# Layer 0 of a four-layer network: a new order of its operations, and the last tile's second-half sums on VectorE

## The chip, the cores and the metric

The kernel runs on one core of a Trainium2 chip. The metric is the device time in microseconds (us) of one execution, lower is better. A core has five engines with a queue each, which run in parallel and wait for each other through semaphores: TensorE (PE, with its weight load PEld), VectorE (DVE), ScalarE (ACT), GpSimd (POOL) and SyncE (SP), which issues most of the DMA transfers here. Every engine works strictly through its own queue: an instruction that waits holds up all that stand behind it.

## The reference

Four layers, each `x = x + layer(groupnorm(x))`, on x of 8 images, 16 channels, 256 x 256. Only layer 0 is touched. It is a capsule convolution with three rounds of routing:

```python
votes = conv3x3(groupnorm(x), w)          # 8 images, 8 atoms x 16 channels each
logits = zeros
for _ in range(3):
    r = softmax(logits, axis=images)
    preds = squash(sum over images, atoms kept: votes * r)
    logits = logits + sum over atoms: votes * preds
return preds
```

`squash(t)` is `n2 * t / ((1 + n2) * sqrt(n2))` with n2 the squared norm of t along its first axis. The softmax runs over the 8 images. Layers 1 to 3 (a spline convolution, an attention over patches, a circular convolution) follow and are the same in both kernels.

## The kernel before, in words

Layer 0 works on 64 tiles of four image rows, all images and channels at once. A tile has two halves, h = 0 and h = 1, of 512 columns for each partition. The first round needs no softmax (its logits are zero), so a tile goes through one squash, and then twice through "logits, softmax, weighted sum, squash". I call these two passes round 1 and round 2. The steps of a tile, with the lines that the profile names:

- Input: SP fetches x (`xs`, L478), PE normalises it (`pd`, two matmuls, L487), ACT moves it out (L490) and its queue puts it in DRAM (`d`, L499). This is made for tile i + 2 in the step of tile i.
- Votes: SP fetches shifted rows back (`kr` and `kt`, L528; `kt` of half 1, L610). Half 0: `cv<-kr` (L557, four matmuls) and `cv<-kt` (L550) for each of two row pairs; half 1: `cv<-kt` (L587 and L591), four operations of four matmuls. ACT copies them to `v` (L572, L596).
- Squash: ACT squares (L641), PE sums (`n`, L645, eight matmuls), ACT (L659 to L661), DVE (L665, L666), ACT (L670, L671), POOL (`times`, L675 to L678).
- Logits, for each half: PE spreads the factor over a PSUM buffer (`fb`, L697), DVE scales (L715) and multiplies twice (`pr`, L723, four and three images), PE sums (`pl`, L733, four and three matmuls). ACT moves `pl` out (L766 in round 1, L755 in round 2, where POOL adds it, L760).
- Softmax: PE transposes (`lg`, L780), DVE (L786, L787), ACT (L792), DVE (L796 to L798), PE transposes back (`rt`, L804), ACT copies (`rs`, L813).
- Weighted sum, for each half: PE spreads the weights in two groups, `rb45`+`r6` (three matmuls, L831) and `rb01`+`rb23` (four matmuls, L831); DVE makes four products `dd` (`dd45`, `dd6`, `dd01`, `dd23`, L842); POOL adds them up in five additions (L851): two of 128x1024 and three of 128x512.
- End: after round 2 a last `fb` for each half, DVE (L893), POOL (L896), ACT statistics (L908), SP stores.

PSUM holds three buffers of the kind "x" (two banks each) and two of the kind "u" (one bank each) for all of these; `pd`, `cv`, `fb` and `rb` each take an x buffer, the others a u buffer. A new use of a buffer waits for the last reader of the old one. So `fb`, for instance, can be held up by DVE still reading an older `rb`.

What comes when is not the order of this list. `work(i)` records each tile's 147 operations (`op`) with what they read and write, and `_Order.run` puts them in one sequence: operation m of tile n has the rank `n * 48 + TIMES[m]`, and among the operations whose predecessors are placed and whose buffers are free in the planner's count, the one of lowest rank comes next. The sequence is then cut up into the engines' queues. A negative entry of about -1000 stands for "as soon as it can". The durations given to `op` (its second argument) are not used by `run`. Two to three tiles are in work at once, so PE's queue for one period holds steps of three tiles.

Of the kernel before, what the change touches and what calls it, by code (L numbers as in the profile page):

```python
# [12 lines left out]
ALU = mybir.AluOpType  # L13
# [10 lines left out]
TILES = H // 4  # L24
# [160 lines left out]
class _Buf:  # L185
# [10 lines left out]


TIMES = [
    -1017.19, 743.46, 708.62, 498.18, -984.65, -996.51, -997.22, 751.01, 751.99, 751.01, 752.12, 750.77,
    -967.35, -903.62, -974.59, 753.99, 754.00, 753.77, 445.66, 393.73, -780.66, -960.80, 755.37, 755.59, 760.20,  # L200
    707.64, 775.69, 780.13, 782.25, 565.91, 658.76, 763.54, 681.24, 605.08, 709.84, 767.15, 644.09, 776.33,
    664.78, 790.04, 756.59, 796.59, 757.08, 765.74, 797.09, 318.31, 799.87, 800.80, 377.30, 696.72, 800.88,
    717.59, 571.56, 737.04, 802.63, 604.46, 530.71, 804.53, 784.88, 636.95, 657.50, 800.06, 517.07, 807.24,
    715.03, 742.15, 830.33, 840.65, 809.85, 812.29, 605.85, 802.98, 816.03, 807.95, 821.83, 824.88, 831.28,
    830.39, 840.66, 789.85, 845.72, 805.49, 748.11, 612.37, 736.06, 636.75, 809.44, 848.88, 838.39, 852.49,
    854.69, 850.98, 859.07, 855.18, 468.16, 857.49, 859.83, 859.02, 698.63, 610.89, 868.22, 704.59, 653.78,
    580.88, 884.00, 654.67, 695.12, 888.80, 889.83, 889.82, 808.47, 890.27, 690.66, 805.44, 696.48, 782.31,
    896.59, 899.53, 896.48, 777.07, 667.15, 682.59, 886.03, 640.00, 674.37, 898.75, 899.76, 887.82, 843.57,
    670.73, 902.64, 828.29, 828.95, 658.08, 885.55, 571.52, 801.95, -872.70, 907.37, 403.39, 814.67, 908.69,
    735.69, 919.60, 844.76, 829.08, -789.01  # L210
]


# [79 lines left out]
class _Net:  # L293
# [123 lines left out]
    def layer0(self, wd, bd, less0, tiles=range(TILES)):  # L417
# [5 lines left out]
        nc, tc = self.nc, self.tc  # L423
        xf = self.d["x"].rearrange("b c h w -> (b c) (h w)")
        last = B - 1
        with ExitStack() as st:
# [23 lines left out]
            for row in (0, H + 1):  # L450
                nc.sync.dma_start(
                    out=self.d0[row * ROW : row * ROW + ROW].rearrange("(p w) -> p w", p=P), in_=ring[0][:, 0, :]
                )
                nc.sync.dma_start(
                    out=self.x1[row and 15, :, :, row and 9, row and 1, :].rearrange("b c w -> (b c) w"),
# [3 lines left out]
                    out=self.x1p[:, row and 1, :, row and H // 2, :], in_=ring[0][:, 0, 0:W]  # L459
# [7 lines left out]
            def buf(kind, shape, name=None):  # L467
                pool = psum if kind in banks else sbuf
                n = {**places, **banks}[kind]
                return _Buf(kind, lambda: pool.tile(shape, F32, name=name or kind, tag=kind, bufs=n))  # L470
# [34 lines left out]
            def work(i):  # L505
# [3 lines left out]
                def op(*a, **k):  # L509
                    ops.append(order.op(*a, **k))  # L510
# [109 lines left out]
                def voted(h, a):  # L620
                    return [(v[h], a // 4, 0), (v[h], a // 4, 1)]
# [8 lines left out]
                def rows(ap):  # L630
                    return ap.rearrange("p (r w) -> p r w", w=W)
# [184 lines left out]
                def weighted(rs):  # L816


                    s = buf("s", [P, 2, 2, W])
                    for h in range(2):  # L820

                        def term(images, h=h):

                            rb = [buf("x", [P, 2, 512], "rb") if len(a) == 2 else buf("u", [P, 1, 512], "r6") for a in images]

                            def products():
                                for pair, r in zip(images, rb):
                                    for n, a in enumerate(pair):
                                        g, j = a // 4, (0, 2, 1, 3)[a % 4]
                                        at = slice(32 * j, 32 * j + 32)  # L830
                                        nc.tensor.matmul(  # L831
                                            r()[:, n], spread[at, g, h, :], rs()[at], start=True, stop=True
                                        )

                            op("PE", 1.25, products, [(rs, 0)], [(r, 0) for r in rb] + [(s, "turn")], mode="r32")
                            out = []
                            for pair, r in zip(images, rb):
                                n, a = len(pair), pair[0]
                                dd = buf("dd", [P, 2, 512])

                                def multiply(n=n, a=a, r=r, dd=dd):
                                    nc.vector.scalar_tensor_tensor(  # L842
                                        dd()[:, :n], r()[:, :n], 1.0 / B, v[h]()[:, a : a + n], ALU.subtract, ALU.mult
                                    )

                                op("DVE", 0.2 + 0.52 * n, multiply, [(r, 0)] + voted(h, a), [(dd, 0)])
                                out.append(dd)
                            return out

                        def add(out, a, b, us):  # L850
                            op("POOL", us, lambda: nc.gpsimd.tensor_tensor(out[0](), a[0](), b[0](), ALU.add),  # L851
                               a[1] + b[1], out[1])

                        d45, d6 = term([(4, 5), (6,)])
                        sh = (lambda h=h: s()[:, :, h], [(s, h)])
                        add(
                            sh,
                            (lambda h=h: rows(v[h]()[:, last]), voted(h, last)),
                            (lambda d=d6: rows(d()[:, 0]), [(d6, 0)]),
                            1.3,  # L860
                        )
                        d01, d23 = term([(0, 1), (2, 3)])
                        both = (d01, [(d01, 0)])
                        add(both, both, (d45, [(d45, 0)]), 2.4)
                        add(both, both, (d23, [(d23, 0)]), 2.4)
                        for n in range(2):
                            add(sh, sh, (lambda d=d01, n=n: rows(d()[:, n]), [(d01, 0)]), 1.3)
                    return s
# [1032 lines left out]
```

## Time and profile before

| what | value |
| --- | --- |
| time, median of 3 runs | 6140.17 us (6139.69 to 6145.74) |
| the profiled execution: time, span | 6146.27 us, 6144.5 us |
| PE busy over the span | 5840.8 us (95%) |
| DVE, ACT, POOL busy | 5267.0 us (86%), 3232.8 us (53%), 3815.2 us (62%) |
| in layer 0, 500 to 1000 us: PE, DVE, ACT, POOL busy of 500 us | 492.7, 454.4, 244.8, 440.2 us |
| the same stretch: granted PE clock, DMA share | 1.00, 0.54 |
| layer 0: first `pd`, last store issued | 100.9 us, 3274.5 us |
| layer 1: first matmul | 3296.9 us |

Layer 0 is thus some 3180 us of 6144. Its first 100 us are statistics of x, the next 150 us fill the pipeline, and from about 238 us the same pattern returns tile after tile until about 3150 us, when no further tile comes in and the engines run dry. A row of the timeline merges instructions of one line and tile that follow each other; the trace has two records for each of these matmuls, so `fb` with four matmuls is shown as x8. Its columns are: start, length, engine, line, operation, output and inputs, shapes, count, and in brackets idle time just ahead with what ended it.

### The profile page before, as it was taken

What the parts mean: (1) busy time and instruction counts of PE and PEld (TensorE: products, weight loads), DVE (VectorE), ACT (ScalarE), POOL (GpSimd) and SP (SyncE); (2) the same over time, 40 slices, a digit from 0 to 9 for tenths busy, and PEclk for the clock granted to TensorE, in tenths of its full rate; (3) what the DMA queues carried; (4) which work ended last, traced back from release to release, by engine and by line L of the source; (5) the groups of instructions that cost most, each with busy time, mean ns of one, the idle gap of its engine ahead of it and who ended that gap; (6) DMA issues with size and microseconds to landing.
All of it is one profiled execution on the core that took longest, in us unless ns stands there. A gap on an engine that the chain in (4) does not pass through costs nothing.

```text
span 6144.5 us, 117856 instructions
## 1 busy us (share of the span) xinstructions
PE 5840.8 (95%) x46024; PEld 2923.2 (48%) x46024; DVE 5267.0 (86%) x6933; ACT 3232.8 (53%) x4986; POOL 3815.2 (62%) x3552
## 2 busy tenths in 40 slices
PE   2999999999999999999976999999999999999998
PEld 0344444444444444444433444444444589999863
DVE  5799999999999999999987999999999877777741
ACT  0444454445444454445435888888888533333321
POOL 0588888888888888888884344434433344444333
PEclk9999999999999999999987999999999999999999
DMA  7455555555555555555524555555556554445458
GB/s 290 117 136 136 127 145 140 137 129 137 143 136 135 130 144 141 136 127 140 135 62 144 185 175 176 178 174 174 179 176 181 159 105 103 95 89 102 113 184 260
DMA packets 581531, 902.51 MB, mean 147 GB/s; under 512 B 292082, under 2 KB 368466, under 8 KB 537586
## 3 DMA queue, kind: packets, MB, share of 16 engines
q1 hardware_dynamic: 537138, 831.69, 49.8%
q10 hardware_dynamic: 33984, 34.08, 1.8%
q0 software_dynamic: 9856, 29.20, 1.6%
q8 instruction: 366, 6.00, 0.4%
q14 instruction: 187, 1.53, 0.1%
HBM read 684.09 MB, written 210.77 MB: 146 GB/s over the span
## 4 chain that ended last, share of the span: by engine, by line
PE 58%; DVE 27%; issue 7%; POOL 3%; DMA 3%; ACT 2%; SPq 0%; DVEq 0%; POOLq 0%; ACTq 0%
PE rb L831 8%; PE cv L587 7%; DVE bases L1089 7%; PE pq L1517 6%; PE pl L733 6%; DVE e L1079 5%; PE cv L591 4%; PE cv L550 4%; PE psc L1585 4%; PE po L1601 4%; PE p L1718 3%; PE pv L1517 3%; DVE pr L723 2%; DVE a L1079 2%; DVE a L1058 2%
## 5 line engine op out<-in xcount | busy, mean ns | idle before, releaser
L1112 PE MATMUL ps<-bases,tw 128*32 128x512 f32 (+1 forms) x13824 | 1360.6, 545 | 16.2 <-POOL bases L1081 6.5
L851 POOL TENSOR_TENSOR dd<-dd 128x1024 f32<-128x1024 f32 x512 | 1212.0, 2367 | 70.1 <-DVE dd L842 64.9
L1081 POOL TENSOR_TENSOR bases<-e,a 128x1024 f32<-128x1024 f32 (+1 forms) x264 | 621.7, 2378 | 926.4 <-DVE e L1079 926.4
L723 DVE TENSOR_TENSOR pr<-v,fb 128x2048 f32<-128x2048 f32 (+1 forms) x512 | 1020.8, 2014 | 17.1 <-PE pl L733 12.5
L1112 PEld LDWEIGHTS ps<-bases,tw 128*32 128x32 f32 x13824 | 597.6, 109 | 800.6 <-issue 484.2
L842 DVE SCALAR_TENSOR_TENSOR dd<-rb,v 128x1024 f32<-128x1024 f32 x768 | 906.8, 1215 | 8.8 <-POOL dd L851 3.3
L851 POOL TENSOR_TENSOR s<-s,dd 128x512 f32<-128x512 f32 x512 | 647.8, 1275 | 15.1
L831 PE MATMUL rb<-rs,ct_fold 32*128 32x512 f32 x3072 | 592.5, 634 | 25.6 <-DVE pr L723 20.1
L851 POOL TENSOR_TENSOR s<-v,dd 128x512 f32<-128x512 f32 x256 | 328.8, 1284 | 292.4 <-DVE dd L842 292.4
L587 PE MATMUL cv<-kt,w 128*128 128x512 f32 x1024 | 498.8, 609 | 11.6 <-DMA kt<-d 10.4
L733 PE MATMUL pl<-pr,ct_fold 128*32 128x512 f32 x3584 | 505.1, 601 | 3.1 <-DVE pr L723 3.1
L550 PE MATMUL cv<-kt,w 128*128 128x512 f32 x1024 | 477.3, 609 | 4.5 <-DMA kt<-d 4.5
L1089 DVE SCALAR_TENSOR_TENSOR bases<-xr,xm,bases 128x1024 f32<-128x1024 f32 (+1 forms) x264 | 446.5, 1729 | 0.3 <-POOL bases L1081 0.3
L596 ACT COPY v<-cv 128x1024 f32<-128x1024 f32 x256 | 251.9, 1008 | 303.3 <-PE cv L591 303.3
L1615 POOL COPY y<-y 128x2 f32<-128x2 f32 x128 | 24.1, 189 | 599.7 <-DVE y L1606 599.7
L1066 ACT ACTIVATE sq<-a 128x1024 f32<-128x1024 f32 (+1 forms) x264 | 263.7, 999 | 231.3 <-DVE a L1058 230.6
L831 PEld LDWEIGHTS rb<-rs,ct_fold 32*128 32x128 f32 x3072 | 226.0, 185 | 325.4 <-issue 129.1
L697 PEld LDWEIGHTS fb<-f,ct_fold 64*128 64x128 f32 x3072 | 208.3, 188 | 309.0 <-issue 176.6
L842 DVE SCALAR_TENSOR_TENSOR dd<-r,v 128x512 f32<-128x512 f32 x256 | 177.0, 692 | 191.3 <-PE r L831 176.8
L572 ACT COPY v<-cv 128x1024 f32<-128x1024 f32 x256 | 258.2, 1009 | 139.4 <-PE cv L550 139.3
L1048 ACT ACTIVATE d<-xr,bd,sd 128x1024 f32<-128x1024 f32 (+1 forms) x264 | 319.1, 1209 | 13.2 <-DMA xr<-x1p 13.2
L550 PEld LDWEIGHTS cv<-kt,w 128*128 128x128 f32 x1024 | 184.6, 190 | 289.1 <-issue 282.3
(320 smaller groups left out, 11365.5 us busy)
## 6 DMA issues: line engine op xcount, KB each, us to landing
xr<-x1p SPq DMA_DIRECT2D x120, 1024.0 KB
kt<-d SPq DMA_DIRECT2D x256, 387.0 KB
kt<-d SPq DMA_DIRECT2D x128, 516.0 KB
d<-dn ACTq DMA_DIRECT2D x64, 516.0 KB
kr<-d SPq DMA_DIRECT2D x128, 258.0 KB
kt<-d SPq DMA_DIRECT2D x128, 258.0 KB
x<-y SPq DMA_DIRECT2D x128, 258.0 KB
xs<-in_x_dram SPq DMA_DIRECT2D x16, 2048.0 KB
```

What stands on the lines that cost most here:

```text
L550: nc.tensor.matmul(ps[g]()[:, n], w[:, 0], t[:, a : a + 2, 0:W], start=False, stop=True)
L587: nc.tensor.matmul(ps()[:, n], w2[:, 0, j, :], t[:, a : a + 2, 0:W], start=True, stop=False)
L723: nc.vector.tensor_tensor(pr()[:, :n].rearrange("p n (r w) -> p n r w", w=W), v[h]()[:, 4 * g : 4 * g + n].rearrange("p n (r w) -> p n r w ...
L733: nc.tensor.matmul(pl()[at : at + 32], sel[:, g, h, :], pr()[:, t, :], start=h == 0 and g == 0, stop=h == 1 and (g == 1 or t == 3),)
L831: nc.tensor.matmul(r()[:, n], spread[at, g, h, :], rs()[at], start=True, stop=True)
L842: nc.vector.scalar_tensor_tensor(dd()[:, :n], r()[:, :n], 1.0 / B, v[h]()[:, a : a + n], ALU.subtract, ALU.mult)
L851: op("POOL", us, lambda: nc.gpsimd.tensor_tensor(out[0](), a[0](), b[0](), ALU.add), a[1] + b[1], out[1])
L1079: nc.vector.tensor_tensor(q, q, part[4 + k], ALU.mult)
L1081: nc.gpsimd.tensor_tensor(ring[n % 3][:, 0, p : p + m, 1 : 1 + W], rows(e), rows(a), ALU.subtract)
L1089: nc.vector.scalar_tensor_tensor(r, rows(part[1]), xm[:, b : b + 1], v, ALU.is_gt, ALU.mult)
L1112: nc.tensor.matmul(out if k is None else out[:, k], lhs, rhs, start=start, stop=stop, skip_group_check=True)
L1517: nc.tensor.matmul(out, lhs, rhs, start=start, stop=stop, skip_group_check=True)
```

## The change

Two edits, both in layer 0. The list `TIMES` gets 147 new numbers, said to be found with the transfers treated as a queue. And in the last tile (i = 63) the five additions of half 1 in each of the two rounds are issued on VectorE in place of GpSimd: ten instructions.

```diff
 TIMES = [
-    -1017.19, 743.46, 708.62, 498.18, -984.65, -996.51, -997.22, 751.01, 751.99, 751.01, 752.12, 750.77,
...
+    812.81, 884.95, 817.92, 666.13, -7133.44, -7210.22, -7230.57, 859.91, 871.57, 872.02, 854.18, 682.23,
...
 ]
...
-                        def add(out, a, b, us):
-                            op("POOL", us, lambda: nc.gpsimd.tensor_tensor(out[0](), a[0](), b[0](), ALU.add),
+                        name, engine = ("DVE", nc.vector) if h and i == TILES - 1 else ("POOL", nc.gpsimd)
+
+                        def add(out, a, b, us, name=name, engine=engine):
+                            op(name, us, lambda: engine.tensor_tensor(out[0](), a[0](), b[0](), ALU.add),
                                a[1] + b[1], out[1])
```

No instruction is added or removed. What the numbers do is seen in the queues that come out of them. In one period of the steady part PE's queue reads, from one `n` of a new tile to the next (the number behind a name is that of its matmuls, and `fb` has four):

```
before: n8 pl7 fb rb4 lg cv4 fb cv4 rt pd rb3 rb4 pl7 fb n8 kr4 kt4 rb3 rb4 pl7 fb lg kr4 kt4 rt
        cv4 rb3 rb4 n8 pl4 fb cv4 rb3 pl3 fb
after:  n4 fb n4 fb rb4 lg cv4 fb cv4 rt rb3 pl4 rb4 pl3 n8 kr4 fb kt4 rb3 rb4 pl7 fb lg kr4 kt4
        rt pd rb3 pl4 rb4 fb n8 pl3 cv4 cv4 rb3 pl7
```

(`kr4`, `kt4` are the operations of L557 and L550, `cv4` one of L587 and L591.) DVE's queue from the product behind the first `rb4` of that list on reads, in order:

```
before: dd01 | softmax | dd23 | softmax | scale pr4 pr3 | dd6 dd45 dd01 dd23 | scale pr3 ...
after:  dd23 | softmax | dd01 | softmax | scale pr4 pr3 | dd6 dd45 dd01 dd23 | f | scale pr4 ...
```

The `fb` that stands behind `pl7` (before) and behind `kr4` (after) there is the factor of half 1 in round 1. Before, its PSUM buffer is the one that `dd45` reads; after, it is the one that `dd23` reads, two products later in DVE's queue. `pd` stands between `rt` of round 2 and the `rb3` that needs its copy before; after, it stands behind `rt` of round 1, and `rt` of round 2 is followed by its own `rb3` at once. On SP, the fetch of `xs` stood at the head of the queue as early as the buffer allowed; now it stands among the others, and at the start of the layer the fetch of tile 1's x stands behind the six `kr` and `kt` fetches of tile 0.

## The prediction

> **What bounds the kernel now.** I read the busy shares in slices first, then the stretches of layer 0, then the timelines of PE and DVE over one tile, last the timelines of the run-out and of layer 1. From 500 to 1000 us PE is busy 492.7 of 500 us at full clock: layer 0 is PE's queue, and no transfer is waited for. The timeline of PE over a steady tile (start, length, ..., idle time ahead):
>
> ```profile
> 1570.99 0.65 PE L645 MATMUL n<-sq,ct_fold 128*32 128x128 f32 x16
> ...
> 1573.92 1.22 PE L831 MATMUL rb<-rs,ct_fold 32*128 32x512 f32 x8
> 1575.46 0.66 PE L780 MATMUL lg<-ct_fold,ls 128*128 128x128 f32 x4 [0.32 <-POOL ls L760]
> ...
> 1588.73 0.72 PE L697 MATMUL fb<-f,ct_fold 64*128 64x128 f32 x8
> 1589.37 0.65 PE L645 MATMUL n<-sq,ct_fold 128*32 128x128 f32 x16
> ...
> 1595.05 0.70 PE L831 MATMUL rb<-rs,ct_fold 32*128 32x512 f32 x2 [0.32 <-DVE pr L723]
> ...
> 1618.58 0.64 PE L645 MATMUL n<-sq,ct_fold 128*32 128x128 f32 x16
> ...
> 1621.50 1.22 PE L831 MATMUL rb<-rs,ct_fold 32*128 32x512 f32 x8
> ```
>
> The same `n` comes back after 1618.58 - 1570.99 = 47.59 us: the period. Cut it at two places: from `rb` x8 to `fb` 1588.73 - 1573.92 = 14.81 us (stretch A), from `fb` to the next `rb` x8 1621.50 - 1588.73 = 32.77 us (stretch B). PE's waits are 0.3 us long and two or three per tile, so there is little to gain: without them all, and with nothing else changed, at most 0.7 us per tile. What can be lost shows on DVE, in the same tile:
>
> ```profile
> 1575.17 1.22 DVE L842 SCALAR_TENSOR_TENSOR dd<-rb,v 128x1024 f32<-128x1024 f32 x1
> ...
> 1581.46 3.95 DVE L723 TENSOR_TENSOR pr<-v,fb 128x2048 f32<-128x2048 f32 x2
> 1585.84 0.69 DVE L842 SCALAR_TENSOR_TENSOR dd<-r,v 128x512 f32<-128x512 f32 x1 [0.42 <-PE r L831]
> 1586.44 3.48 DVE L842 SCALAR_TENSOR_TENSOR dd<-rb,v 128x1024 f32<-128x1024 f32 x3
> ```
>
> From 1575.17 to 1589.92 DVE has one pause, of 0.42 us. Today `fb` at 1588.73 waits for none of it: its buffer is free after `dd45`, the first of the three, at about 1587.66. The pause and this early release are what keeps DVE off PE's path.
>
> **The new order, stretch A.** In the new queue the same `fb` follows `kr4`, and its PSUM buffer is read last by `dd23`, the third of the three. DVE's row from the first `dd` to `dd23` keeps its members (first `dd`, softmax, second `dd`, softmax, scale, two multiplies, four `dd`), only the two first `dd` change places. Lay it out from the rows: `rb` x8 starts, the first `dd` 1.25 us later (1575.17 - 1573.92), the multiplies end 1585.41 - 1575.17 = 10.24 us after that, then the four `dd` take 1589.92 - 1585.84 = 4.08 us, without the pause, since `rb3` is now early. That is 15.57 us, less 0.08 of overlap, plus 0.05 to 0.15 for the hand-over (0.15 is how far `rb` at 1595.05 starts behind the end of its `pr`): A = 15.6 us, 0.8 more than today. What PE itself has to do there is less than before, since `pd` (1.81 us) has moved out: by its rows 14.3 us. So PE stands still for 1.3 us of A. Part of this is visible as a second wait. `rt` of round 2 is now followed by its own `rb3`, with no `pd` to cover ACT's copy. The rows of the run-out, where there is no `pd` left, price it:
>
> ```profile
> 3152.25 0.65 PE L804 MATMUL rt<-ct_fold,e 128*128 128x128 f32 x4
> 3153.93 0.70 PE L831 MATMUL rb<-rs,ct_fold 32*128 32x512 f32 x2 [1.03 <-ACT rs L813]
> ```
>
> There the copy waits some 0.35 us for ACT's previous copies; without these the idle time is 0.7 us. It lies inside A, so it is not added: if DVE were not late, it alone would remain. What is late next: behind `fb` on PE stand `kt4`, `rb` and all else, so the whole period shifts.
>
> **Stretch B.** It loses `n8` (1589.37 to 1589.95, 0.58) and `kr4` (1.08), which go to A, and gains `pd` (1.81): 32.77 - 0.58 - 1.08 + 1.81 = 32.92. The wait of 0.32 at 1595.05 falls away, but the `rb` behind such a wait run some 0.4 us faster (seven take 1.92 us there and 2.33 at 1584.55), so that gives nothing. New: `pl` and `rb` are cut into each other three times in a tile, and PE's queue has 45 runs for 43. `pl` as 4 and 3 takes 0.97 + 0.99 us where 7 take 1.85, so a cut costs 0.1; `rb` as 3 and 4 takes 1.06 + 1.22 against 2.30, so nothing. A second `rb` waits for ACT's copy out of `kt` (1.01 us and two hand-overs, against 0.96 us of PE work): 0.15. B = 32.92 + 0.1 to 0.5; I take 33.1. Between kinds of matmul that never follow each other in this trace the bounds are -0.3 (the cuts overlap) and +0.5; the row nearest to them, the cut `pl`, says 0.1 each.
>
> A + B = 48.7 us, against 47.59: **+1.1 us per tile**, bounds +0.4 (B at 32.6, and the bank free 0.3 earlier) and +1.5. Some 60 tile steps run so: +66 us.
>
> **Transfers.** In the steady part the fetches keep their lead: `kt` is fetched when its buffer is left by PE, and the new SP order puts nothing in front that waits longer than 18 us before the use; a burst of them took 7 us here. Cost nothing; if that cover went, every us late would be a us per tile. At the start SP's group `xs` x3 (97.05 us, 15.03 long) becomes one `xs`, six fetches that wait for tile 0's `d`, and only then tile 1's x: its fetch goes out near 113 us instead of 104.6, so its `pd` is 8 or more us later. Against that, tile 0's votes no longer stand behind the third `pd` (3.78 us at 115.05), and the fetch of half 1 no longer behind the put of tile 2, whose landing at 133.3 us held it. I take 0, bounds -6 and +8.
>
> **The last tile.** Ten additions go from POOL to DVE. POOL's rows in the run-out are 2.37 us (1024) and 1.28 us (512); for each round 2 x 2.37 + 3 x 1.28 = 8.6 us. DVE has no such row; the nearest are `dd` at 1.21 and `fb<-s,fb` at 0.69: 2 x 1.21 + 3 x 0.69 = 4.5 us. In round 2 of tile 63 POOL's chain runs from 3245.31 to 3263.30, 18 us, and the end waits for it. With both engines at once the end of half 1 would come near 3257.5, 5.8 us earlier. But these additions read two SBUF tiles, and in this trace such a DVE instruction does not run beside POOL's. Layer 1, two equal instructions:
>
> ```profile
> 3499.76 2.32 DVE L1089 SCALAR_TENSOR_TENSOR bases<-xr,xm,bases 128x1024 f32<-128x1024 f32 x1
> ...
> 3502.77 1.28 DVE L1089 SCALAR_TENSOR_TENSOR bases<-xr,xm,bases 128x1024 f32<-128x1024 f32 x1
> 3498.61 2.39 POOL L1081 TENSOR_TENSOR bases<-e,a 128x1024 f32<-128x1024 f32 x1
> ```
>
> The first has POOL beside it until 3501.00 and takes 2.32 us, the second has POOL idle and takes 1.28 us; L1079, with one operand in PSUM, takes 1.21 us either way. So 8.6 + 4.5 us go one after the other with about 1 us of waits: 14 us for 18, 4 us gained, and about as much in round 1, where POOL's queue is full from 3187 to 3223. I take -8, bounds 0 and -14.
>
> [...]
>
> **Sum.** +66 + 0 - 8 = +58 us. The profiled execution took 6146.27 us (span 6144.5 and 1.8 around it), so 6204 us; it lies 6.1 us above the median, and on the median of 6140.17 the forecast is **6198 us**, 1% slower. Bounds together: 60 x 0.4 - 6 - 14 = +4, and 60 x 1.5 + 8 = +98: 6144 to 6238.
>
> **Rivals.**
> - DVE is not the bound of A (the buffer is free earlier than the queue says), and only the uncovered `rs` copy remains: 0.7 of idle time less 0.2 that faster `rb` give back, +0.5 per tile; +30 - 8 = +22, 6162 us. For it: DVE's row has 1.3 us of play only by my sum of PE rows. Against: the hand-over is in the new queue. Chance 0.2; it lies in the range.
> - Faster: the waits of today vanish and no new one comes; PE runs at its rows. A at 14.3 plus B at 32.7 would be 47.0, -0.6 per tile: -36 - 8 = -44, 6096 us. It needs `dd23` to end 1.3 us sooner after `rb` x8 and the `rs` copy to be covered; it decides from A + B below 47.4. Against it: DVE's 15.6 us are rows, no estimates. For it: kinds of matmul in a sequence that the trace never shows. Chance 0.10.
> - No change: a period within 0.2 of today's, which A's excess and cheaper cuts could give, with the ends: about 6140. Chance 0.06.
> - The start goes wrong: tile 1's late x costs 8 to 15 us on top of the main case, 6210; in the range.
>
> Main case 0.64 and the first rival 0.2 are both slower by more than 0.2% (12 us, about what a measurement of this kernel can tell from no change). Faster 0.10, same 0.06, slower 0.84.
>
> **What would show it.** Right: a period near 48.7 us; PE idle before `fb` (L697), released by DVE `dd` L842, some 0.2 to 0.6 us in each tile, and before `rb` (L831), released by ACT `rs` L813, 0.7 us; POOL's chain at the end some 4 us shorter with DVE additions (L853) longer than 1.21 us; PE busy below 97% in the steady part. Wrong: a period at or below 47.6, or PE idle mainly on transfers.

## The result, and the profile after

| what | before | after |
| --- | --- | --- |
| median of 4 runs each, us | 6140.67 (6139.69 to 6145.74) | 6176.38 (6173.73 to 6181.34) |
| ratio to before | 1 | 1.0053, 95% interval 1.0041 to 1.0065 |
| span of the profiled execution, us | 6144.5 | 6171.9 |
| steady period, us | 47.59 | 48.05 |
| stretch A, stretch B, us | 14.81, 32.77 | 15.50, 32.54 |
| tile 2's `n`, us | 237.9 | 242.4 |
| tile 60's `n`, us | 2999.2 | 3028.2 |
| tile 63's `n`, us | 3141.0 | 3171.7 |
| last operation of layer 0 ends, us | 3276.1 | 3306.4 |

The change makes the kernel 0.53% slower. The lower rows say where: layer 0 ends 30.3 us later. Of these, 4.5 us are lost before tile 2's `n`, 24.5 us over the next 58 tile steps (0.42 us each in the mean), 1.7 us in the three steps after them, and 0.4 us come back behind tile 63's `n`. The layers behind, which are the same, took 2.9 us less in this execution than in the one of before.

PE's timeline over the same tile as in the prediction (start, length, engine, line, operation, output and inputs, shapes, count, idle time ahead and what ended it):

```profile
1586.80 0.41 PE L645 MATMUL n<-sq,ct_fold 128*32 128x128 f32 x2
...
1589.43 1.14 PE L831 MATMUL rb<-rs,ct_fold 32*128 32x512 f32 x8
...
1597.69 0.66 PE L804 MATMUL rt<-ct_fold,e 128*128 128x128 f32 x4
1599.03 0.70 PE L831 MATMUL rb<-rs,ct_fold 32*128 32x512 f32 x2 [0.68 <-ACT rs L813]
...
1601.09 1.14 PE L831 MATMUL rb<-rs,ct_fold 32*128 32x512 f32 x8
...
1603.58 1.35 PE L557 MATMUL cv<-kr,w 32*128 32x512 f32 x8
1604.93 0.72 PE L697 MATMUL fb<-f,ct_fold 64*128 64x128 f32 x8
...
1634.84 0.41 PE L645 MATMUL n<-sq,ct_fold 128*32 128x128 f32 x2
```

and DVE's in the same tile:

```profile
1600.81 0.68 DVE L842 SCALAR_TENSOR_TENSOR dd<-r,v 128x512 f32<-128x512 f32 x1
1601.41 3.47 DVE L842 SCALAR_TENSOR_TENSOR dd<-rb,v 128x1024 f32<-128x1024 f32 x3
...
1605.70 0.70 DVE L715 TENSOR_TENSOR fb<-v,fb 128x512 f32<-128x512 f32 x1 [0.43 <-PE fb L697]
```

The period is 1634.84 - 1586.80 = 48.04 us; A is 1604.93 - 1589.43 = 15.50. `fb` starts at 1604.93, 0.05 us behind the end of DVE's third `dd` (`dd23`, 1604.88), and yet no idle time stands ahead of it. The `kr` ahead of it was held up too: its row is 1.35 us long, where the same operation later in the tile takes 1.14. `kr` takes two PSUM buffers, and its third matmul, the first into the second buffer, starts at 1603.81, 0.06 us behind the end of `dd01` (1603.75). So PE waits for two of DVE's products in a row, and none of it is listed as idle time: a wait can lie inside a row, between the matmuls of one operation.

PE's waits from 1000 to 1500 us (us in total, times, longest), first before, then after:

```profile
PE lg L780 <- POOL ls L760: 3.6, 11, 0.3
PE rb L831 <- DVE pr L723: 3.5, 11, 0.3
```

```profile
PE rb L831 <- ACT rs L813: 6.7, 10, 0.7
```

Two waits of 0.32 us per tile have gone, and one of 0.68 has come. Such a list holds only the idle time between rows. Before had a hidden wait as well, in a `kr` of stretch B; PE's and DVE's rows there, then the same `kr` after:

```profile
1600.17 1.42 PE L557 MATMUL cv<-kr,w 32*128 32x512 f32 x8
...
1596.94 3.48 DVE L842 SCALAR_TENSOR_TENSOR dd<-rb,v 128x1024 f32<-128x1024 f32 x3
```

```profile
1614.69 1.14 PE L557 MATMUL cv<-kr,w 32*128 32x512 f32 x8
```

Before, the third matmul of this `kr` starts at 1600.47, 0.05 us behind the end of a `dd23` (1600.42); after, it is not held up. PE's work in a tile can thus not be had by taking the listed waits off the period. What changed in stretch B shows when every row is taken from its own start to the start of the next, so that waits are included (us, medians over the tiles from 600 to 2600 us):

| rows of stretch B | before | after |
| --- | --- | --- |
| first `kt`, the idle 0.32 us (before) and the seven `rb` behind it | 5.94 | 5.91 |
| the `kr` shown above | 1.35 | 1.07 |
| second `kt`, `rt` | 4.14 | 3.97 |
| the other ten `rb` | 3.36 | 3.20 |
| `cv` of half 1, twice | 5.85 | 5.95 |
| `pl` and `n`, 21 and 16 matmuls | 6.55 | 6.69 |
| `fb` five times, `lg` | 3.93 | 3.93 |
| `n8` and `kr4`, which go to A (before), `pd` (after) | 1.66 | 1.81 |

### The profile page after: what moved, and what is told of

Its sections match the earlier page's. It is cut to its first block, busy times and chain, and to the rows that moved or that the text cites. A ratio compares the mean times of both kernels' runs of the same rounds, so it can differ in the third digit from the quotient of the medians.

```text
span 6171.9 us, 118027 instructions
## 1 busy us (share of the span) xinstructions
PE 5845.4 (95%) x46024; PEld 2864.8 (46%) x46024; DVE 5293.9 (86%) x6943; ACT 3238.0 (52%) x4986; POOL 3817.4 (62%) x3542
## 4 chain that ended last, share of the span: by engine, by line
PE 51%; DVE 23%; POOL 16%; issue 5%; DMA 3%; ACT 2%; SPq 0%; POOLq 0%; ACTq 0%; DVEq 0%
PE cv L550 7%; DVE bases L1091 7%; PE rb L831 7%; PE pq L1519 6%; POOL dd L853 5%; PE pl L733 5%; DVE e L1081 4%; POOL s L853 4%; PE psc L1587 4%; PE po L1603 4%; PE p L1720 3%; PE pv L1519 3%; PE cv L557 2%; DVE a L1081 2%; DVE a L1060 2%
## 5 line engine op out<-in xcount | busy, mean ns | idle before, releaser
L853 POOL TENSOR_TENSOR dd<-dd 128x1024 f32<-128x1024 f32 x508 | 1199.4, 2361 | 101.6 <-DVE dd L842 81.7
L733 PE MATMUL pl<-pr,ct_fold 128*32 128x512 f32 x3584 | 522.3, 607 | 4.6 <-DVE pr L723 4.3
L587 PE MATMUL cv<-kt,w 128*128 128x512 f32 x1024 | 504.9, 615 | 9.5 <-DMA kt<-d 9.4
L550 PE MATMUL cv<-kt,w 128*128 128x512 f32 x1024 | 473.7, 605 | 2.5 <-issue 2.5
L831 PEld LDWEIGHTS rb<-rs,ct_fold 32*128 32x128 f32 x3072 | 162.5, 184 | 381.9 <-ACT rs L813 108.8
L1081 DVE TENSOR_TENSOR a<-a,sq 128x1024 f32<-128x1024 f32 (+1 forms) x264 | 312.3, 1183 | 2.3 <-ACT sq L1068 2.3
L1081 DVE TENSOR_TENSOR e<-e,sq 128x1024 f32<-128x1024 f32 (+1 forms) x264 | 312.3, 1183 | 0.0
```

The costliest lines, as they stand in the source:

```text
L550: nc.tensor.matmul(ps[g]()[:, n], w[:, 0], t[:, a : a + 2, 0:W], start=False, stop=True)
L587: nc.tensor.matmul(ps()[:, n], w2[:, 0, j, :], t[:, a : a + 2, 0:W], start=True, stop=False)
L733: nc.tensor.matmul(pl()[at : at + 32], sel[:, g, h, :], pr()[:, t, :], start=h == 0 and g == 0, stop=h == 1 and (g == 1 or t == 3),)
L831: nc.tensor.matmul(r()[:, n], spread[at, g, h, :], rs()[at], start=True, stop=True)
L853: op(name, us, lambda: engine.tensor_tensor(out[0](), a[0](), b[0](), ALU.add), a[1] + b[1], out[1])
L1081: nc.vector.tensor_tensor(q, q, part[4 + k], ALU.mult)
```

## The experiments

In some runs the planner's finished sequence is edited before it goes into the queues. An entry `([(a, m)], where, k, q)` puts operation m of tile n + a behind or ahead of operation q of tile n + k, for n from 5 to 59. Where there is no entry, the sequence is the planner's own.

**1. Is it DVE's chain that holds `fb`?** `dd6` of half 0 in round 2 is made twice:

```diff
-                                    nc.vector.scalar_tensor_tensor(
+                                    for _ in range(2 if last_round and h == 0 and n == 1 else 1):
+                                        nc.vector.scalar_tensor_tensor(
```

> The new order, and in each tile VectorE makes the product dd6 of half 0 in round 2 twice (0.61 us more; the values are the same). DVE has some 4 us of play per tile, so this costs something only where DVE is the bound. Theory (stretch A is set by DVE's unbroken chain up to dd23, which fb waits for): all of it is seen, A 15.5 + 0.6 = 16.1 us, period 48.65 us, time 6176 + 60 x 0.6 = 6212 us, ratio 1.011. Rival (the first rival of the prediction: only the uncovered rs copy holds PE in A, fb's buffer is free in time): period 48.05 us, 6176 us, ratio 1.005.

Measured: 6223.65 us, ratio 1.0128 (1.0113 to 1.0144), period 48.77. DVE's timeline of the doubled product:

```profile
1620.90 1.41 DVE L843 SCALAR_TENSOR_TENSOR dd<-r,v 128x512 f32<-128x512 f32 x2
```

It takes 1.41 us for 0.69, and the period grows by the same 0.72. On PE it is the `kr` ahead of `fb` that gets longer, from 1.36 to 2.08 us from its start to that of `fb`. DVE has 4 us of pauses in each tile, none of them on this stretch. So DVE's chain decides when PE gets to `fb`. The opposite, a chain made shorter, with VectorE scaling 64 columns of 512:

```diff
-                            nc.vector.tensor_tensor(p()[:, :, 0:W], s(h), p()[:, :, 0:W], ALU.mult)
+                            r, c = (1, 64) if h == 0 and before is None else (2, W)
+                            at = p()[:, 0:r, 0:c]
+                            nc.vector.tensor_tensor(at, s(h)[:, 0:r, 0:c], at, ALU.mult)
```

> The new order; VectorE scales only 64 of the 512 columns of fb for half 0 in round 1 (L715), so that its chain in stretch A is some 0.55 us shorter. The rest of that scaling is left out of the computation. Theory (DVE's chain up to dd23 holds fb some 0.3 us beyond the time at which PE, with its wait of 0.68 us on the rs copy, would be there): A falls from 15.50 to 15.2 us and the period to 47.75 us, no further, since PE's own row then sets it. Rival (only the rs copy is felt): period 48.05 us.

Measured: period 47.84, A 15.31 (a single execution took 6167.04 us, one of before beside it 6155.15). DVE's timeline of this run in A:

```profile
1591.84 0.22 DVE L717 TENSOR_TENSOR fb<-v,fb 128x64 f32<-128x64 f32 x1
...
1597.96 2.35 DVE L844 SCALAR_TENSOR_TENSOR dd<-rb,v 128x1024 f32<-128x1024 f32 x2 [0.18 <-PE rb L833]
```

0.47 us are saved on DVE and 0.20 are seen. The rest stands as a pause of 0.18 ahead of `dd01`, which now waits for PE's second `rb`. So two rows lead to `fb` and are within 0.2 us of each other: DVE's chain, and PE's own, `rs` copy, `rb3`, `pl4`, `rb4`, then `dd01` and `dd23`. I had looked for 0.30, with PE's row ending at `kr` and not in these two `dd`.

**2. Can the uncovered `rs` copy be covered again?** `pd` goes back between `rt` of round 2 and its `rb`:

```diff
+MOVES = [([(1, 0)], 'behind', -3, 143), ([(1, 1)], 'ahead', -2, 107), ([(1, 2), (1, 3)], 'behind', 0, 29)]
```

> The new order, but in the steady part pd (with its fetch of x and its copy) stands where it stood before: between rt of round 2 and the rb that needs the copy. Theory (PE's work is 46.9 us per tile in both kernels; after has 1.16 us of waits: 0.68 on the rs copy of round 2, some 0.3 on dd23 ahead of fb, 0.18 elsewhere; before has 0.69): the two waits of round 2 go, but the rs copy of round 1, which pd covered, comes out with 0.67: period 46.9 + 0.67 + 0.18 = 47.75 us, time near 6158 us, ratio 1.003. Rival 1 (the rs copy of round 2 is the whole loss, that of round 1 hides behind other work): 47.1 to 47.4 us, 6119 to 6137 us. Rival 2 (DVE's chain up to dd23 sets the stretch whatever PE does in it, and the cuts of pl and rb cost the rest): no better than 48.0 us, 6176 us.

Measured: 6191.5 us, ratio 1.0075 (1.0059 to 1.0090), period 48.32: slower than after, on the side of rival 2. PE's and then ACT's timeline of this run, further on in the tile:

```profile
1627.20 0.60 PE L824 MATMUL rt<-ct_fold,e 128*128 128x128 f32 x4
1628.96 0.70 PE L851 MATMUL rb<-rs,ct_fold 32*128 32x512 f32 x2 [1.15 <-ACT rs L833]
...
1627.40 1.01 ACT L592 COPY v<-cv 128x1024 f32<-128x1024 f32 x1 [0.70 <-PE cv L570]
1628.31 0.59 ACT L833 COPY rs<-rt 128x512 f32<-128x512 f32 x1
```

The copy of round 1, which `pd` had covered, now costs 1.15 us, since ACT is at a copy of `cv` when `rt` ends. And in A `pd` pushes the second `rb` back by a microsecond, `dd23` ends 0.8 us later, and A grows to 16.29 us. The next run takes away the part that is ACT's:

```diff
+MOVES = [([(1, 0)], 'behind', -3, 143), ([(1, 1)], 'ahead', -2, 107), ([(1, 2), (1, 3)], 'behind', 0, 29), ([(1, 19)], 'behind', 0, 56)]
```

> As the run with pd moved back, and ACT copies rs of round 1 ahead of the second copy of cv, behind which it stood (34.40 against a rt that ended at 33.89, in a tile's own time). That run had a period of 48.32 us with 1.15 us of idle time ahead of the rb of round 1. Theory (the copy waited 0.5 us for ACT): the idle time falls to 0.67 and the period to 47.85 us. Rival (PE would wait as long elsewhere, since the second copy of cv now comes 0.6 us later, or DVE's chain sets the period): 48.2 us or more.

Measured: period 48.30 (a single execution took 6182.80 us). The wait fell from 1.15 to 0.67 as said, and the period did not follow: it came back as waits for DVE, 0.21 us ahead of the second `rb` of round 1, whose buffer a `pr` still reads, and for POOL's `f`, 0.28 us ahead of an `fb`. With a second cover, `cv` behind `rt` of round 1:

```diff
+MOVES = [([(1, 0)], 'behind', -3, 143), ([(1, 1)], 'ahead', -2, 107), ([(1, 2), (1, 3)], 'behind', 0, 29), ([(1, 22)], 'ahead', 0, 57), ([(1, 23)], 'behind', -2, 129)]
```

> As the run with pd moved back, and the first cv of half 1 (2.94 us of PE work) is moved between rt of round 1 and the rb that needs its copy. Theory: both rs copies are covered, PE has 46.9 us of work and 0.1 to 0.4 us of waits: period 47.0 to 47.3 us, time near 6120 us, ratio 0.997, faster than both kernels. Rival (DVE's dd behind that rb now start 2.1 us later and DVE has only 4.2 us of play per tile, so DVE or its hand-overs set the period): 47.6 us or more, 6149 us or slower.

Measured: 6284.48 us, ratio 1.0223 (1.0209 to 1.0237), 49.84 us per tile in the mean. PE's waits from 1000 to 1500 us of this run:

```profile
PE fb L717 <- POOL f L698: 18.3, 17, 1.6
```

Both copies are covered and none of their waits is left, but the `dd` of round 1 come later, POOL's additions and its `f` behind them too, and PE waits for that instead. Both fills put PE work ahead of an `rb` and with it delayed DVE, which had none to spare there. The last run joins this case and the shorter DVE chain:

> The run with pd moved back and rs of round 1 copied first (period 48.30 us), with the same scaling of 64 of 512 columns, the rest of it left out of the computation. Theory (in that run DVE's chain sets the period, in A and behind fb, and PE follows it): nearly all of the 0.55 us is seen, 47.75 to 47.9 us. Rival (PE's wait of 0.67 us on the copy and its own row set it, DVE has play): 48.2 us or more.

Measured: period 48.75 (a single execution took 6210.92 us). By its number that is the rival's side, but the shorter chain made it slower than without, which neither side has a reason for. Of PE's waits from 1000 to 1500 us one is new, that of `rb` for DVE's `pr`, 0.36 us in each tile. In this build `rb3` was given the PSUM buffer that the second `pr` still reads, where in the run before it was the next `rb` that got it. The order of the operations is the same, the choice of buffers is not. Inconclusive.

**3. What does a cut of `pl` cost?**

```diff
+MOVES = [([(-2, 90)], 'ahead', -2, 92)]
```

> The new order, but in stretch B one of the cuts is undone: the pl of tile n-2 that stands as 4 and 3 with rb4, fb and n between goes out as 7 behind n. Theory (a cut costs nothing; stretch B was 32.55 us because the removed wait of 0.32 us was saved in full): the period does not fall; the rb that moves up waits 0.1 us for DVE's pr, so 48.05 to 48.2 us. Rival (the prediction's term, 0.1 us for each cut): 47.95 us.

Measured: period 48.29 (a single execution took 6191.65 us), 0.25 more with one cut less, which is more than either side expected. Of PE's waits from 1000 to 1500 us a new one:

```profile
PE rb L851 <- DVE pr L743: 1.8, 11, 0.2
```

Taken from start to start, `n8` and `pl7` in one take 2.28 us where the cut rows took 2.42, so the cut by itself costs 0.14 us, close to the prediction's 0.1. But the two `rb` that now follow each other take 2.52 us in place of 2.14: the `pl4` between them had given DVE the time to free the second one's buffer. Of these 0.39 us only 0.16 per tile (1.8 over 11) are listed as a wait. The net is the 0.25. The theory's reason, that the wait of 0.32 us had been saved in full, does not hold either: by the first row of the table above it gave 0.03.

**4. The start.** Tile 1's x is fetched ahead of tile 0's rows. The edit moves one operation, once:

```diff
+    o = at[(-1, 143)]
+    line.remove(o)
+    line.insert(line.index(at[(0, 14)]), o)
```

> The new order, but at the start of the layer the fetch of tile 1's x is put ahead of tile 0's kr and kt fetches on SP. Theory (this fetch alone makes the start late): its pd comes near 111 us in place of 127.4, the first votes of half 1 near 147 us in place of 154.2, tile 2's n near 238 us in place of 242.4; time 6176 - 4.5 = 6172 us. Rival (the third x, which the last kt fetch of tile 0 stands behind, or the burst of fetches takes it back): tile 2's n still at 240 us or later, 6174 us or more. The steady period stays at 48.05 us.

Measured: 6158.07 us, ratio 1.0020 (1.0011 to 1.0029), steady period 48.04. PE's timeline of the start, after and then this run:

```profile
127.36 3.78 PE L487 MATMUL pd<-xs,wd 128*128 128x512 f32 x4 [23.17 <-DMA xs<-in_x_dram]
...
154.19 3.75 PE L587 MATMUL cv<-kt,w 128*128 128x512 f32 x4 [9.39 <-DMA kt<-d]
```

```profile
107.80 3.65 PE L510 MATMUL pd<-xs,wd 128*128 128x512 f32 x4 [3.29 <-DMA xs<-in_x_dram]
...
141.30 1.96 PE L610 MATMUL cv<-kt,w 128*128 128x512 f32 x4 [1.38 <-DMA kt<-d]
```

The mechanism is the expected one, its size is not: tile 2's `n` comes at 226.8 us, 15.6 earlier than after and 11.1 earlier than before. One misplaced fetch had hidden that the rest of the new start is much the better one.

**5. The last tile.** The additions alone, in each of the two orders:

```diff
-                        name, engine = ("DVE", nc.vector) if h and i == TILES - 1 else ("POOL", nc.gpsimd)
+                        name, engine = "POOL", nc.gpsimd
```

> The new order of operations, with the ten additions of the last tile back on POOL. Theory (from the trace of after: from the first dd of round 1 in the last tile to the end of the layer takes 68.2 us with DVE additions, 73.1 us in the kernel before): the DVE additions save about 5 us, and the new order loses about as much ahead of that stretch. Then this kernel is 5 us slower than after, near 6181 us (ratio to before 1.0066), and that stretch takes 73 us. Rival (additions on DVE and POOL exclude each other, so that nothing is saved, and the shorter stretch comes from the new order): no change, 6176 us, stretch 68 us. In both the steady period stays at 48.05 us.

Measured: 6174.79 us, ratio 1.0046 (1.0034 to 1.0059), not to be told from after. From tile 63's `n` to the end of the layer it takes 136.4 us, after 134.7.

```diff
-    812.81, 884.95, 817.92, 666.13, -7133.44, -7210.22, -7230.57, 859.91, 871.57, 872.02, 854.18, 682.23,
...
+    -1017.19, 743.46, 708.62, 498.18, -984.65, -996.51, -997.22, 751.01, 751.99, 751.01, 752.12, 750.77,
```

> The old order of operations, with the ten additions of the last tile on DVE. Theory: 5 us faster than before, 6136 us (bounds 2 to 8 us faster), steady period 47.59 us, and the stretch from the first dd of round 1 in the last tile to the end of the layer 68 us in place of 73.1. Rival (the exclusion eats the gain): 6140 us, stretch 73 us.

Measured: 6150.02 us, ratio 1.0005 (0.9996 to 1.0014); the same stretch takes 139.8 us, before 135.1: longer, not shorter. I had compared the stretch from one row to the end across two orders, and laid a difference of the orders at the additions' door. Taken by rounds, in us (round 1 from tile 63's `n` to the first `dd` of round 2, round 2 from there to the start of the last `n`):

| run | order, additions on DVE | round 1 | round 2 |
| --- | --- | --- | --- |
| before | old, none | 103.6 | 19.5 |
| all ten, old order | old, ten | 111.1 | 16.7 |
| five, old order (below) | old, round 2 | 105.9 | 16.7 |
| five, old order, new start (below) | old, round 2 | 102.8 | 16.7 |
| back on POOL | new, none | 103.6 | 20.75 |
| after | new, ten | 105.2 | 17.5 |
| tile 1's x first | new, ten | 103.7 | 17.5 |

Round 2 gains 2.8 and 3.3 us. Round 1 gains nothing, and in the old order loses some 5 to 8 us. DVE's timeline there, in the run with the old order:

```profile
3199.85 0.70 DVE L787 TENSOR_TENSOR lg<-lg,e 128x512 f32<-128x512 f32 x1
...
3201.59 2.48 DVE L853 TENSOR_TENSOR dd<-dd 128x1024 f32<-128x1024 f32 x2
3204.10 0.69 DVE L853 TENSOR_TENSOR s<-s,dd 128x512 f32<-128x512 f32 x1
3204.71 0.68 DVE L796 TENSOR_REDUCE e<-lg 128x64 f32<-128x512 f32 x1
```

The additions stand in the middle of the other chain's softmax, 3.2 us of them between its two steps (L787, then L796), and the rest of that chain waits for it. What makes up the remainder of the 5 to 8 us is not shown. So only round 2:

```diff
-                        name, engine = ("DVE", nc.vector) if h and i == TILES - 1 else ("POOL", nc.gpsimd)
+                        name, engine = ("DVE", nc.vector) if h and i == TILES - 1 and last_round else ("POOL", nc.gpsimd)
```

> The old order, with the additions of the last tile's half 1 on DVE in round 2 alone (five instructions). In the run with all ten on DVE, round 2 of the last tile got 2.8 us shorter (from its first dd to the last n 16.7 us against 19.5) and round 1 7.5 us longer, since they stood in front of DVE's softmax. Theory: layer 0 ends 2.8 us earlier after tile 63's n than before (132.3 us against 135.1), time 6140.7 - 3 = 6138 us, ratio 0.9995, too little for these intervals. Rival (the gain of round 2 was only what round 1 had lost): 135 us.

Measured: 6142.22 us, ratio 0.9997 (0.9989 to 1.0006). Round 2 has the 2.8 us, but the end comes 134.6 us after tile 63's `n`: round 1, whose order is that of before, took 2.3 us longer (more on this below).

**6. What is good of it, on the old order.** The five additions as in the run before, and the start in the manner of run 4:

```diff
+    o = at[(0, 0)]
+    line.remove(o)
+    line.insert(line.index(at[(0, 13)]) + 1, o)
...
```

In the same way operation (0, 1) is put behind (0, 16), (0, 2) behind (0, 18), (0, 3) behind that, and (1, 0) behind (1, 4): the third x, its `pd`, copy and put stand behind tile 0's votes of half 0, and the fourth x behind tile 1's first rows.

> The old order in the steady part, additions of the last tile's half 1 on DVE in round 2 alone, and at the start the order of the run with tile 1's x first: two x fetches, then tile 0's kr and kt fetches, and the third x with its pd behind tile 0's votes. Theory (with the start as in that run, whose first votes of half 1 came at 141.3 us against 147.1 before): 6 to 11 us saved at the start and 3 in the last tile: tile 2's n near 230 us in place of 237.9, time ratio 0.998 to 0.9985, faster than both kernels. Rival (the fill of the old order waits for the third x, whose pd now comes some 20 us later): tile 2's n at 237 us or later, ratio 0.9995 or more.

Measured: 6136.31 us, ratio 0.9989 (0.9980 to 0.9998): faster than before by a tenth of a percent (the interval ends at 0.9998), between theory and rival. Tile 2's `n` is at 233.7 us (4.2 earlier than before, less than the 6 looked for), the period 47.59, and the end 131.5 us after tile 63's `n`.

## Why the prediction was right and where it was wrong

The sign, and the reason for it, held: slower, since A grows by DVE's chain and by a copy that nothing covers. Forecast +58 us; layer 0 in the traces shows +30, the medians +36. Term by term:

- *PE bounds layer 0, at most 0.7 us per tile to gain.* The 0.7 counts the idle time between PE's rows; the `kr` of before holds another 0.28 inside its row. No run here had a period below 47.59 us, so what there is to gain stays open.
- *A = 15.6 us.* Right: 15.50, and the two runs of experiment 1 show that DVE's chain sets it, so the first rival's reason (`fb`'s buffer is free in time, only the copy is felt) falls, though its +0.5 per tile is close to the measured 0.45. What I missed is that PE's row through `rb4` and the two last `dd` is only 0.2 us shorter: the 14.3 us of its rows left out the wait for the copy. And `kr4`, which moved ahead of `fb`, waits for `dd01` on its own.
- *B = 33.1 us.* This is the term that was mis-sized: 32.54. The sum reached 32.92 by moving operations and added 0.1 to 0.5; the rows give 0.4 less than 32.92. The largest piece is `kr`: the one that leaves was taken at 1.08, and the other was left at the 1.35 of before, which held a wait for DVE that the new order does not have (0.28 us). The ten other `rb`, one pair of them now cut by `pl`, took 0.16 less, where the sum put nothing, and the second `kt` with `rt` 0.17 less. The cuts of `pl` and `n` cost 0.14 in all (the sum had 0.1 each), and `cv` took 0.10 more. The wait of 0.32 was rightly booked as no gain: 5.94 us with it, 5.91 without. With B at 32.5 and A as forecast the period would have been 48.1, and the sum 60 x 0.5 = +30 in place of +66.
- *Start 0, bounds -6 and +8.* The net of +4.5 lies inside, but it is +15.6 from tile 1's x and -11.1 from the rest (run 4). I had put the late `pd` at 8 us or more; it came 19.4 us later than before.
- *Last tile -8.* Measured -0.4 for the whole run-out. In round 2 the additions save 3.3 us in this order (forecast 4), while DVE's and POOL's hold each other up (2.21 us for 0.69, 3.98 for 2.61), as the forecast had read it from the two rows of layer 1 (2.32 us for 1.28). "About as much in round 1" is the step that failed: I saw a full POOL queue and did not ask what the end of that round waits for, which is DVE's softmax.
- *What would show it.* The idle time ahead of `rb` came as said (0.68 against 0.7). The one ahead of `fb` is not listed, since the `kr` ahead of it was held up by DVE as well, and PE's busy share from 500 to 1000 us is 98.2% (490.9 of 500), not below 97%: such a share counts a wait inside a row as work.

Part of the miss cancelled by luck: the steady part was forecast 40 us too long (66 against 26), the start and the last tile together 12 us too short.

## What to carry to other kernels

Here two engines hand work back and forth, and the period followed the ring and not the busier engine's sum: before filling a gap on one engine, follow what the fill delays on the other. Add a known time to a suspected chain and see whether the period takes all of it; this settled in one run what the idle columns did not show. And ask of work moved off a full queue what its stage ends with, for a queue that is full is not always waited for.

## What the runs showed of the hardware

In round 2 of the last tile the additions on DVE and POOL held each other up, in both directions. DVE's and POOL's timelines there, in after:

```profile
3282.99 2.21 DVE L853 TENSOR_TENSOR s<-v,dd 128x512 f32<-128x512 f32 x1
...
3286.37 1.23 DVE L853 TENSOR_TENSOR dd<-dd 128x1024 f32<-128x1024 f32 x1
...
3279.88 4.77 POOL L853 TENSOR_TENSOR dd<-dd 128x1024 f32<-128x1024 f32 x2 [1.00 <-DVE dd L842]
3284.73 3.98 POOL L853 TENSOR_TENSOR s<-s,dd 128x512 f32<-128x512 f32 x2
```

DVE's addition of 512 columns, 0.69 us when alone, takes 2.21 while POOL's runs on to 3284.65. Then POOL's pair, 2.61 us elsewhere, takes 3.98: 1.37 more, with DVE's addition of 1.23 us inside.

In the run-out the same order does not take the same time. The two runs with the additions of round 2 alone, with the old start and with the new, have the same order of operations there, and need 134.6 and 131.5 us from tile 63's `n` on. The windows of each, twenty us at the same place, 28 us behind that `n` (stretch, its length, then the busy time of PE, PEld, DVE, ACT and POOL, granted clock, DMA share, GB/s), old start first:

```profile
3168.00:3188.00 20.00, 13.80 (x88) 5.87 (x82) 15.17 (x16) 4.40 (x10) 14.63 (x12) 0.70 0.00 1
```

```profile
3164.70:3184.70 20.00, 13.10 (x93) 5.80 (x90) 17.05 (x18) 4.41 (x10) 15.95 (x13) 0.83 0.00 1
```

and one operation in it, by PE's timeline, old start first:

```profile
3181.60 1.85 PE L733 MATMUL pl<-pr,ct_fold 128*32 128x512 f32 x8
```

```profile
3177.13 1.25 PE L768 MATMUL pl<-pr,ct_fold 128*32 128x512 f32 x8
```

PE stands still for 4.34 us ahead of an `rt` in the one and for 4.32 in the other, the granted clock of the window is 0.70 and 0.83, and the same `pl` takes 1.85 and 1.25 us. That the clock makes the whole difference is not shown, but a gain of 3 us in the run-out is no more than the 3.1 us by which these two runs differ there; the round 2 column above, equal to a tenth of a microsecond between runs of one order, is the better measure.
